# A graph layer and a GAT layer on one core: all rows of the second layer turned by VectorE, and ScalarE's opening order set by hand

## The chip, the cores and the metric

The kernel runs on one core of one Trainium2 chip. The time is device time in microseconds; the median of three runs of the kernel before is 937.41 us (936.95 to 938.42). The profiled execution that all rows below come from spans 936.6 us.

## The reference

There are 4096 nodes with 512 features. Layer 0 is attention inside 32 graphs of 128 nodes each (the tiles of the kernel), with the dense matrix `adj` standing for both biases; layer 1 is a graph attention layer with 8 heads over the edges `adj > 0`. Both are pre-norm with a residual:

```python
h = relu(layernorm(x))
q, k, v = h @ Wq.T + bq, h @ Wk.T + bk, h @ Wv.T + bv
a = where(same_graph, q @ k.T * scale, 0)
x = x + (softmax((a + adj + adj) * where(same_graph, 1, -1e6)) * same_graph) @ v

h = relu(layernorm(x))
mx = einsum('nf,hfd->hnd', h, W)                 # 8 heads of 64
t = einsum('hnd,hd->hn', mx, a_dst)              # s_i cancels in the softmax over j
attn = softmax(where(adj > 0, s_i + t_j, -inf))  # over j
x = x + concat_heads(attn @ mx)
```

So layer 1 is, for each node i, the sum over its neighbours j of exp(t_j) * mx_j, divided by the sum of exp(t_j). The kernel computes for each tile j of 128 nodes one "part", the weighted rows and their weights, split in a high and a low half for speed, and then multiplies the 0/1 mask with all 32 parts.

## The kernel before

It has three stages. Layer 0 walks over 16 groups of two tiles. In passing it reads all of `adj` (64 half-row tiles of 1 MB), sums exponentials of the entries outside the graph on ScalarE (`junk`), and lets VectorE write the mask as bytes to memory (`a_d`). A middle stage makes the parts of the tiles that layer 0 has not made yet. The aggregation multiplies masks and parts.

The opening folds the query and key weights into one matrix, `m_sb`:

```python
bq_sb = const.tile([P, KC], F32, name="bq_sb")
nc.scalar.dma_start(bq_sb, bq)
bk_sb = const.tile([P, KC], F32, name="bk_sb")
nc.scalar.dma_start(bk_sb, bk)
# ... (in fold)
wkT_sb = load_weight(tmp, wkT, "wkT_sb", KC, tag="lo")
wqT_sb = load_weight(tmp, wqT, "wqT_sb", KC, tag="lo")
loads()                       # first rows, wv, bv (ScalarE's queue), adjacency tiles
# ...
for n, wT in enumerate((wkT_sb, wqT_sb)):
    for k in range(KC):
        for m in range(KC):
            nc.tensor.transpose(pt[:, m, :], wT[:, k, ts(m, P)], ident)      # L198
        nc.scalar.copy(w[:, :, ts(k, P)], pt)
        if n == 0 and k == 0:
            rows = [spread_bias(b) for b in (bk_sb, bq_sb)]                  # L184
# ... VectorE: u_col, c_sb, zk from the weights and the bias rows
for m in range(KC):
    if m == 2: ...            # u_sb, z_sb (L224, L230)
    if m == 3: first()        # norm and turn the first two tiles
    for k in range(KC):
        nc.tensor.matmul(pp, wq[:, k, ts(m, P)], wk[:, k, :], ...)           # L236
    nc.scalar.mul(m_sb[:, m, :], pp, SCALE)                                  # L239
```

Then come `values` (L473) for the first two tiles, the reading of adjacency rows 0 and 1 (`read`: mask on VectorE, `junk` on ScalarE, own block on GpSimd) and `queries` (L461).

The rows of layer 1 (the output of layer 0, stored in `x1_d`) must be normalised, passed through a ReLU and transposed before the projection. Tiles 0 to 15 are transposed on TensorE:

```python
def relu_T(ps_pool, hn, dst):
    pt = ps_pool.tile([P, KC, P], F32, name="pt")
    for k in range(KC):
        nc.tensor.transpose(pt[:, k, :], hn[:, ts(k, P)], ident)             # L136
    nc.scalar.activation(dst, pt, AF.Relu)                                   # L137
```

Tiles 16 to 31 (`MIXED = NT // 2`) are transposed in 32 by 32 blocks by VectorE; four tiles share one block buffer, go to memory in one store, and come back with the blocks in place:

```python
def turn(i):
    c, b = divmod(i, BY)
    if b == 0:
        blocks[c] = sb4.tile([P, P // B, KC, BY, B], F32, name="blocks")
    nc.vector.transpose(blocks[c][:, :, :, b], rows[i].rearrange(...))       # L655
    if b == BY - 1:
        nc.sync.dma_start(hT_d[c], blocks[c]...)

def move(c):
    hT = sb5.tile([P, P // B, KC, P], F32, name="hT4")
    for q in range(P // B):
        nc.sync.dma_start(hT[ts(q, B)]..., hT_d[c, :, q]...)
    for u in range(BY):
        hTs[c * BY + u] = hT[:, u]
```

The projection and the weighting of one tile:

```python
def project1(ps_m, hT, w1x):
    pm = [ps_m.tile([P, D], F32, name="pp") for _ in range(2)]
    for g, n in ((1, HW + H), (0, HW)):
        for k in range(KC):
            nc.tensor.matmul(pm[g][:, :n], hT[:, k, :], w1x[:, k, g * HW : g * HW + n], ...)  # L264
    return pm
# weigh (L273, VectorE): e = pm * exp(t); split: high half (ScalarE), low half (GpSimd)
```

Layer 0's loop, cut to its order:

```python
for g in range(NG):                      # NG = 16
    s = scores(g, hT, gT, r, *look)      # L519
    prepare_on(last)
    if not last:
        ngT = queries(nhT)               # L461
    sT = turned(s)                       # L538
    prepare_on(3 <= g and g % 2)         # turn one row tile, project the one before
    for _ in range(...): begin1()        # fetch and norm a row tile
    for t in range(G):
        look_on(t)                       # read adjacency rows of group g + 1
        if not last and t == 0: nvs.append(values(nhT, t))
        attend(sT, vs[t], g, t)          # L546, writes x1_d
        prepare_on(last and t == 0)
        if not last and t: nvs.append(values(nhT, t))
    if g + 2 < NG:
        nhT, hns = turned0(g + 2)        # L136 for layer 0's own rows
        nr = row_terms(hns)
```

In the middle stage, for tiles below 16, TensorE turns the next row, and ScalarE weighs half of the tile in four pieces (L724); from 16 on VectorE weighs both halves. Rows to be turned by VectorE are taken up `AHEAD = 8` tiles before their projection; a move is issued three tiles before its first use.

## Time and profile before

| what | value |
|---|---|
| median time | 937.41 us |
| opening, to the first values product | 29.2 us |
| layer 0's groups | to about 355 us |
| middle stage (tiles 8 to 31) | 355.4 to 442.8 us |
| aggregation and end | 442.8 to 936.6 us |
| VectorE busy, 45 to 345 us | 204.74 us |
| ScalarE busy, 45 to 345 us | 175.93 us |
| DMA, 45 to 345 us | share 0.80, 308 GB/s |

The busy times come from the profile's table of windows. A DMA share of 1 means that all 16 DMA engines had packets the whole time. In the listings below a line gives the engine, the source line (L136), the operation, what it writes and reads, shapes, how often, and in brackets how long the engine stood idle before it and what released it; PE is TensorE, PEld its weight load, DVE VectorE, ACT ScalarE, POOL GpSimd, SP SyncE. A float32 product appears as two instructions, a transpose as one. The transposes by VectorE, and the costliest stores, in the page's columns (group, busy us and mean ns, idle before; for transfers the size and the median us from issue to landing):

```profile
L655 DVE STREAM_TRANSPOSE blocks<-rowm 128x512 f32<-128x512 f32 x16 | 11.2, 698 | 6.6 <-ACT rowm L730 6.5
a<-adj SPq DMA_DIRECT2D x64, 1024.0 KB, 12.2
a_d<-a SPq DMA_DIRECT2D x32, 512.0 KB, 10.3
hT_d<-blocks SPq DMA_DIRECT2D x4, 1024.0 KB, 4.6
hT<-hT_d SPq DMA_DIRECT2D x16, 256.0 KB, 5.2
```

### The profile page before, as it was taken

To read this page: it belongs to the slowest core of one execution; us is meant where nothing else is said; L and a number is where in the kernel's file an instruction comes from. 1 tells how busy PE (TensorE), PEld (TensorE's weight loads), DVE (VectorE), ACT (ScalarE), POOL (GpSimd) and SP (SyncE) were. 2 spreads that over 40 slices of the span, in tenths; PEclk is the share of its full clock that TensorE was granted. 3 is DMA by queue.
4 is the path that set the end of the run, shared out by engine and by line. 5 is a ranking of instruction groups with operands and counts; after the bars stand their busy time and mean duration, and the time that the engine had idled before them with its cause. 6 is when DMAs were issued, how large, how long until landed. Compare 5 with 4: busy or idle time off the path is not lost.

```text
span 936.6 us, 13145 instructions
## 1 busy us (share of the span) xinstructions
PE 925.9 (99%) x4987; PEld 809.1 (86%) x4987; DVE 462.2 (49%) x992; ACT 268.1 (29%) x539; POOL 180.4 (19%) x344
## 2 busy tenths in 40 slices
PE   8999999999999999999999999999999999999997
PEld 5676677767677778888999999999999999999997
DVE  4678878777775447754463324242424233332412
ACT  4876576667672216532000000000000000000000
POOL 1311212331221116654101010110101010101010
PEclk9999999999999999999999999999999999999999
DMA  9999997989997114764123131312121222313111
GB/s 334 415 382 401 349 351 302 360 344 371 356 354 273 35 35 146 203 200 103 53 61 91 46 90 46 90 51 85 52 85 54 82 71 65 88 48 90 46 45 37
DMA packets 61062, 156.63 MB, mean 167 GB/s; under 512 B 6722, under 2 KB 23490, under 8 KB 52290
## 3 DMA queue, kind: packets, MB, share of 16 engines
q1 hardware_dynamic: 51058, 138.70, 42.9%
q10 hardware_dynamic: 9936, 17.05, 4.9%
q8 instruction: 40, 0.66, 0.3%
q14 instruction: 28, 0.23, 0.1%
HBM read 117.97 MB, written 37.75 MB: 166 GB/s over the span
## 4 chain that ended last, share of the span: by engine, by line
PE 94%; DMA 3%; ACT 2%; DVE 0%; SPq 0%; issue 0%; ACTq 0%
PE pg L315 51%; PE pp L264 12%; PE pp L461 11%; PE pp L473 11%; PE pp L546 3%; PE pss L519 3%; DMA a<-adj 2%; PE pt L136 2%; ACT junk L496 1%; PE pl L315 1%; DMA bv_sb<-bv 1%; PE pss L538 0%; ACT m_sb L239 0%; ACT gT L465 0%; DVE x L548 0%
## 5 line engine op out<-in xcount | busy, mean ns | idle before, releaser
L315 PE MATMUL pg<-part,ata 128*128 128x348 f32 (+1 forms) x1536 | 246.7, 321 | 0.0
L315 PEld LDWEIGHTS pg<-part,ata 128*128 128x128 f32 x1536 | 244.5, 188 | 0.1
L315 PE MATMUL pg<-part,atb 128*128 128x348 f32 x1472 | 236.4, 321 | 0.0
L315 PEld LDWEIGHTS pg<-part,atb 128*128 128x128 f32 x1472 | 234.2, 188 | 0.1
L329 ACT COPY tot<-pg 128x522 f32<-128x522 f32 x31 | 18.6, 600 | 453.4 <-PE pg L315 453.4
L496 ACT ACTIVATE junk<-a 128x2048 bf16<-128x2048 f32 (+15 forms) x92 | 124.5, 1353 | 36.3 <-DMA a<-adj 15.1
L264 PE MATMUL pp<-w1x,hT 128*128 128x256 f32 (+1 forms) x512 | 114.9, 383 | 0.5 <-DVE e L273 0.5
L473 PE MATMUL pp<-wv,hT 128*128 128x512 f32 x256 | 115.0, 593 | 0.3 <-ACT hT L137 0.3
L461 PE MATMUL pp<-hT,m_sb 128*128 128x256 f32 x512 | 113.2, 379 | 0.0
L301 DVE CAST atb<-at 128x4096 fp32r<-128x4096 fp8e4 x16 | 36.7, 2293 | 152.2 <-PE pg L315 152.2
L264 PEld LDWEIGHTS pp<-w1x,hT 128*128 128x128 f32 x512 | 96.0, 190 | 15.0 <-issue 0.9
L461 PEld LDWEIGHTS pp<-hT,m_sb 128*128 128x128 f32 x512 | 96.1, 190 | 12.9 <-issue 0.5
L301 DVE CAST ata<-at 128x4096 fp32r<-128x4096 fp8e4 (+1 forms) x17 | 36.8, 2167 | 140.4 <-PE pg L315 140.3
L146 DVE TENSOR_SCALAR a<-a 128x512 fp8e4<-128x512 f32 x256 | 96.8, 457 | 5.7 <-DMA a_d<-a 5.7
L473 PEld LDWEIGHTS pp<-wv,hT 128*128 128x128 f32 x256 | 47.8, 190 | 54.9 <-issue 53.1
L767 POOL COPY den_all<-tot 128x1 f32<-128x1 f32 x31 | 5.8, 186 | 365.0 <-DVE tot L330 365.0
L771 POOL TENSOR_TENSOR tot<-tot,row 128x512 f32<-128x512 f32 x31 | 39.9, 1288 | 62.2 <-DVE tot L335 58.1
L248 POOL TENSOR_TENSOR part<-e,part 128x522 fp32r<-128x522 f32 x32 | 41.1, 1285 | 12.9 <-ACT part L245 12.7
L122 POOL TENSOR_SCALAR ve<-mv 128x1 f32<-128x1 f32 x64 | 16.3, 259 | 131.1 <-DVE mv L120 131.0
L137 ACT ACTIVATE hT<-pt 128x512 f32<-128x512 f32 x48 | 26.9, 596 | 50.8 <-PE pt L136 40.5
L477 DVE TENSOR_TENSOR v<-pp,bv_sb 128x512 f32<-128x512 f32 x32 | 22.0, 687 | 39.2 <-PE pp L473 39.2
L292 DVE STREAM_TRANSPOSE at<-mw 128x1024 f32<-128x1024 f32 x32 | 39.6, 1238 | 2.1 <-DMA mw<-a_d 2.1
(113 smaller groups left out, 698.4 us busy)
## 6 DMA issues: line engine op xcount, KB each, us to landing
a<-adj SPq DMA_DIRECT2D x64, 1024.0 KB, 12.2
a_d<-a SPq DMA_DIRECT2D x32, 512.0 KB, 10.3
mw<-a_d SPq DMA_DIRECT2D x128, 128.0 KB, 3.9
row<-x_d SPq DMA_DIRECT2D x41, 256.0 KB, 3.5
xg<-x SPq DMA_DIRECT2D x16, 512.0 KB, 5.1
x_d<-x ACTq DMA_DIRECT2D x32, 256.0 KB, 4.3
out<-tot ACTq DMA_DIRECT2D x31, 256.0 KB, 3.7
rowm<-x_d SPq DMA_DIRECT2D x16, 256.0 KB, 5.2
```

The source lines that it names most:

```text
L146: nc.vector.tensor_scalar(a8v[:, u], av[:, u], 0.0, None, ALU.is_gt, saturate=False)
L248: nc.gpsimd.tensor_sub(dst[:, :, 1, :], e3, dst[:, :, 0, :].bitcast(F32))
L264: nc.tensor.matmul(pm[g][:, :n], hT[:, k, :], w1x[:, k, g * HW : g * HW + n], start=(k == 0), stop=(k == KC - 1),)
L292: nc.vector.transpose(at8.rearrange("p c n b -> p (c n b)").bitcast(F32).rearrange("p (c u n) -> p c u n", c=NW, n=B), mw.rearrange("p u ( ...
L301: nc.vector.tensor_copy(at[:, c0 * BY : c1 * BY].rearrange("p (c b) q -> p c b q", b=BY), at8[:, c0:c1].rearrange("p c q b -> p c b q"),)
L315: nc.tensor.matmul(pg[:, : 2 * CW1].rearrange("p (s w) -> p s w", s=2)[:, :, :n], at[:, j, :], part(j)[:, c, :, :n], start=(j == 0), stop= ...
L461: nc.tensor.matmul(pp[:, : G * P], m_sb[:, k, ts(m, P)], hT[:, k, :], start=(k == 0), stop=(k == KC - 1),)
L473: nc.tensor.matmul(pp, hT[:, k, ts(t, P)], wv[:, k, :], start=(k == 0), stop=(k == KC - 1))
L496: nc.scalar.activation(junk[:, c0:c1], a[:, c0:c1], AF.Exp, scale=2.0 * NEG, accum_out=sums[:, n : n + 1],)
L519: nc.tensor.matmul(pss[:, t, :], gT[:, k, ts(t, P)], hT[:, k, ts(t, P)], start=(k == 0), stop=(k == KC - 1),)
L546: nc.tensor.matmul(po, sT[:, t, :], v, start=True, stop=True)
L771: nc.gpsimd.tensor_add(num, num, row)
```

## The change

All 32 row tiles of layer 1 are now turned by VectorE through memory, so that TensorE makes no transposes for layer 1. The first sixteen are turned inside layer 0: each group fetches a row tile at its start and takes it up at its end, one turn after the fetch could be used; stores and moves are placed by hand in chosen groups; the projections inside layer 0 sit in groups 7, 8, 9, 10 and 13 and three in the last. The order of TensorE in layer 0's groups is the program's. To make room, some of layer 0's buffers go from two to one (`gT`, `s`, `sT`) or from three to two (`diag`), and one of the seven adjacency tiles lives in a pool that stays on. In the opening the biases are loaded by SyncE behind the first weight (the value bias behind the value weight), TensorE runs ten transposes of the identity before the weights, the bias rows are spread after all of the first weight's transposes, and ScalarE's instructions follow the program's order until the first values, with the reading of adjacency rows 0 and 1 placed among the last products of the fold. The attention dot products of layer 1's weight (`dots`) are spread over four groups. `AHEAD` goes from 8 to 9. The branch for general inputs, which these inputs do not take, is adapted to the same row order.

```diff
-MIXED = NT // 2
-AHEAD = 8
+AHEAD = 9
+WARM = 10
@@
-    nc.scalar.dma_start(bq_sb, bq)
-    nc.scalar.dma_start(bk_sb, bk)
@@ mask_bytes
-        order = ("p (c b u q) -> p u c b q", "p (c u b q) -> p u c b q")[h]
-        av = a.rearrange(order, c=NW // 2, b=BY, q=B)
+        av = a.rearrange("p (c u b q) -> p u c b q", c=NW // 2, b=BY, q=B)
@@ fold
         wkT_sb = load_weight(tmp, wkT, "wkT_sb", KC, tag="lo")
+        nc.sync.dma_start(bk_sb, bk)
+        nc.sync.dma_start(bq_sb, bq)
         wqT_sb = load_weight(tmp, wqT, "wqT_sb", KC, tag="lo")
@@
+        pt = ps_t.tile([P, KC, P], F32, name="pt")
+        for _ in range(WARM):
+            nc.tensor.transpose(pt[:, 0, :], ident, ident)
@@
-                if n == 0 and k == 0:
+                if n == 0 and k == KC - 1:
                     rows = [spread_bias(b) for b in (bk_sb, bq_sb)]
@@ new: turning inside layer 0
+            keep = prep.enter_context(
+                tc.tile_pool(name="keep", bufs=1, side="right", reuse_waits="tile")
+            )
+            def turn(i, row, pool):
+                c, b = divmod(i, BY)
+                if b == 0:
+                    blocks[c] = pool.tile([P, P // B, KC, BY, B], F32, name="blocks")
+                nc.vector.transpose(blocks[c][:, :, :, b], row.rearrange(...))
+            def store(c): ...
+            def move(c):
+                hT = keep.tile(
+                    [P, P // B, KC, P], F32, name="hT4", tag="a" if c and c % 2 == 0 else "hT4"
+                )
+                ...
+            def fetch(i):
+                rows[i] = sb2.tile([P, D], F32, name="row1")
+                nc.sync.dma_start(rows[i], x1_d[i])
+            def begin(i):
+                norm(rows[i], rows[i])
+                nc.scalar.activation(rows[i], rows[i], AF.Relu)
+                turn(i, rows[i], keep)
@@ opening
+                def between(m, after):
+                    if m == 2 and not after:
+                        first.append(normed0(0))
+                        look[2].append(read(0, look[0][:, 0, :], look[1][0]))
+                    if m == 3 and not after:
+                        first.extend(turned0(0, first.pop()))
+                    if m == 3 and after:
+                        look[2].append(read(1, look[0][:, 1, :], look[1][1]))
+
+                with tc.manual_schedule(engines={mybir.EngineType.Activation}):
+                    m_sb, c_sb, u_sb, z_sb = fold(wp, lo, sb, ps_t, ps_p, loads, between)
@@ layer 0's loop
+                with tc.manual_schedule(engines={mybir.EngineType.PE}):
+                    for g in range(NG):
+                        for i in (g - 1, g) if last else (g - 1,) if g else ():
+                            fetch(i)
+                        if g in (6, 11, 14):
+                            move((6, 11, 14).index(g))
+                        ...
+                        if 2 <= g < 2 + KC:
+                            dots(g - 2)
+                        ...
+                        if g in (7, 8, 9, 10, 13, NG - 1):
+                            prepare()
+                        for t in range(G):
+                            look_on(t)
+                            if t == 0 and g in (5, 9, 13):
+                                store(g // BY - 1)
+                            ...
+                        for i in (g - 1, g) if last else (g - 1,) if g else ():
+                            begin(i)
+                store(LO // BY + 1)
@@ middle stage: every tile as the tiles from 16 on were
-                    if i + 1 < MIXED:
-                        hTs[i + 1] = sb2.tile([P, KC, P], F32, name="hT1")
-                        relu_T(ps_t, rows[i + 1], hTs[i + 1])
+                    if far <= NT:
+                        turn(far - 1, rows[far - 1], (keep, sb4)[(far - 1) // BY % 2])
+                        if far % BY == 0:
+                            store(far // BY - 1)
-                    if i < MIXED:
-                        halves = (0,)
-                        for h in range(H // 2, H):
-                            nc.scalar.mul(...)
```

## The prediction

> **What bounds the kernel now.** I read the page's busy shares first, then TensorE's own list of waits, then its instructions in order of time for the opening, for layer 0's groups and for the stage in between, because a share of 99% says only that the other engines cost nothing as long as they stay ahead. From the page:

> ```profile
> span 936.6 us, 13145 instructions
> PE 925.9 (99%) x4987; PEld 809.1 (86%) x4987; DVE 462.2 (49%) x992; ACT 268.1 (29%) x539; POOL 180.4 (19%) x344
> ```

> TensorE's idle time is 936.6 − 925.9 = 10.7 us. Its waits by releaser (total us, times, longest):

> ```profile
> PE pt L198 <- DMA wkT_sb<-wkT: 3.9, 1, 3.9
> PE pp L264 <- DVE e L273: 0.5, 1, 0.5
> PE pp L236 <- ACT m_sb L239: 0.3, 1, 0.3
> PE pp L473 <- ACT hT L137: 0.3, 1, 0.3
> ```

> That is 5.0 us; the remaining 5.7 us are the end, where the last product is evacuated, scaled and stored. Between 45 and 345 us TensorE is busy 299.86 of 300. So a gain must come from work taken off TensorE or from the opening, and everything added elsewhere is free only while TensorE still finds its data ready.

> The opening, TensorE in order of time (start, length, instructions, idle before):

> ```profile
> 3.92 1.08 PE L198 MATMUL pt<-ident,wkT_sb 128*128 128x128 f32 x4 [3.92 <-DMA wkT_sb<-wkT]
> 4.80 1.91 PE L184 MATMUL pp<-ident,bk_sb 128*128 128x128 f32 x8
> 6.51 1.91 PE L184 MATMUL pp<-ident,bq_sb 128*128 128x128 f32 x8
> 8.21 2.00 PE L198 MATMUL pt<-ident,wkT_sb 128*128 128x128 f32 x12
> 10.12 2.63 PE L198 MATMUL pt<-ident,wqT_sb 128*128 128x128 f32 x16
> 12.59 7.03 PE L236 MATMUL pp<-w,w 128*128 128x512 f32 x16
> ...
> 29.23 7.13 PE L473 MATMUL pp<-wv,hT 128*128 128x512 f32 x16 [0.29 <-ACT hT L137]
> ```

> Eight bias products take 6.51 − 4.80 = 1.71 us, 0.21 each; the same shape at 19.46 us (the row u, line 224) takes 0.89 for eight, 0.11 each. So TensorE works at half rate until about 8.9 us. From 12.59 to 29.23 lie 16.64 us, of which the work is 16.0 and waits for ScalarE 0.6.

> The stage between the layers, where layer 1's rows become weighted parts:

> ```profile
> 355.44 3.67 PE L264 MATMUL pp<-w1x,hT 128*128 128x264 f32 x16
> 358.95 0.60 PE L136 MATMUL pt<-ident,rown 128*128 128x128 f32 x4
> 359.39 3.67 PE L264 MATMUL pp<-w1x,hT 128*128 128x264 f32 x16
> ...
> 379.12 35.23 PE L264 MATMUL pp<-w1x,hT 128*128 128x264 f32 x160
> 414.86 28.29 PE L264 MATMUL pp<-w1x,hT 128*128 128x264 f32 x128 [0.51 <-DVE e L273]
> ```

> From start to start a tile costs 3.51 us of projection and, if TensorE turns it, 0.44 us for four transposes (359.39 − 358.95). The tiles from 379.12 on are turned by VectorE: no transposes.

> [...] first work at 3.92, full rate near 8.9. [...] VectorE's price is one transpose of 128x512 (0.698 us in this trace) and two transfers of 1 MB per four tiles. [...] with weights and biases on two queues the transfer rate falls to 131 GB/s between 4 and 5 us, with the engines still 64% busy. What can help is the order: weights first.

> **The change part by part.**
> (a) Transposes of layer-1 rows 0 to 15 leave TensorE: 16 tiles x 4 = 64 instructions. The trace has them as 36 of tile row (layer 0) and 28 of rown (after it). At 0.437/4 = 0.109 us each: 64 x 0.109 = 7.0 us, all on the bound engine, since it has no gap on either side. Nine tiles' share is inside layer 0 (3.9 us), seven tiles' after it (3.1 us).
> (b) VectorE gets 16 transposes of 0.70 us = 11.2 us, all in layer 0; seven more rows of statistics and normalising there (0.68 + 0.17 + 0.55 = 1.4 us each) = 9.8 us. Between 45 and 345 us it is busy 204.7 of 300 us (68%); with 21 more, 226 (75%). After layer 0 it loses those seven rows and gains the second half of the weighting for eight tiles (8 x 0.41 = 3.3 us, which ScalarE did in four pieces each, 0.93 us). ScalarE's ReLU merely changes its source: 0.60 us from PSUM, 0.63 from SBUF. All this lies beside TensorE: 0 us if it keeps ahead.
> (c) Transfers: four stores and three moves of 1 MB each and seven more rows of 256 KB come into layer 0, some 9 MB. The 308 GB/s x 300 us there are 92 MB; in the busiest windows at a DMA share of 0.99 to 1.02 the rate was 385 to 420. So the load goes from 0.80 to about 0.88: fits. The last adjacency tile is issued at 278.8 us and its users need it after 307, so 20 us of slack stand against some 22 us of transfer spread over 250.
> (d) The opening. The ten warm-up transposes can start when the identity is made (1.24 + 0.29 = 1.53 us) and, at 0.22 us cold, end at 3.8, before the first weights at 3.92: no cost, and 2.3 us of activity earlier. Biases behind the first weight mean that TensorE does the wkT transposes first. I estimate: wkT turned by 6.7 us, bias products done by 8.5, wqT transposes, paced by arrival, done by 10.5 in place of 12.5. Then 16.0 us of work, now with the two ScalarE waits (0.6 us) gone, because the order by hand puts m_sb and hT ahead of the mask sums of tile 1. That gives first values at about 26.5 in place of 29.2: 2.7 us. If transposes do not warm the clock, the bias products still run cold from 7.4 to 10.8 and only the 0.6 us and a little remain: 0.4. I weigh these 7 to 3: 2.0 us.
> (e) AHEAD 9 issues each four-tile move one tile (3.5 us) earlier. The 0.51 us stop at 414.86 is put down to VectorE's e, but the four PSUM tiles hold two tiles' products, so tile 24 needs tile 22's weighting, which ended at 411.3; I take it for a late move: gone, 0.5 us.
> (f) TensorE's order by hand in the groups: the trace already shows program order in every group (queries, turned scores, values, two attends, values), so 0. The mask's first half is read in the second half's order; its 256 operations last 0.45 us in either, so 0.
> (g) The aggregation, 3072 matmuls at about 159 ns, and the end: unchanged.
> Sum: 7.0 + 2.0 + 0.5 = 9.5 us; minus 0.2 for friction: 937.4 − 9.3 = 928.1, rounded to 928.

> **The rivals.**
> *The blocks buffer stops VectorE.* In layer 0 the turned blocks have one buffer: row 4's transpose must wait until the 1 MB store of rows 0 to 3 has been read. The store is placed in the middle of a group and the next transpose at its end, some 10 us later; layer 0's 512 KB mask stores take 10.3 us to land by the transfer table. VectorE works in order, so a wait there delays the v additions that free PSUM for TensorE. Against it: VectorE waited 39.2 us in layer 0 for TensorE's values, so it is that far ahead in places. If it bites at each of the three reuses plus row 16's, 1 to 3 us each: 931 to 936.
> *SyncE's queue is held by a move.* It waits for its store to land, and adjacency loads stand behind it. Seven half-row tiles are in flight, about 1.7 groups of 20 us, against a hold of some 10. If it bites: 2 to 4 us lost, 930 to 932.
> *The clock stays cold*: as in (d), 929.5.
> *VectorE becomes the pace after layer 0.* Tiles 8 to 15 now run at 3.51 us instead of 3.95 with all work on VectorE. In tiles of that kind before, it is busy 6.2 of 7.0 us in one window and 3.9 of 7.1 in the next, with a 2.2 us wait for a row every four tiles; TensorE did not stop for ten tiles. If it drifts over 15 tiles: 1 to 3 us lost.

> **Range and chances.** All gains are small beside 937: the most I can add is 7.0 + 3.9 (TensorE starting its products at 10 and never waiting) + 0.5, which gives 926.0, or 925.2 with the runs' own spread of some 0.8 us; two rivals together give 932. The eight-in-ten range is 925.2 to 931.8, longer above because every rival adds. Over 2% faster means under 918.7, which would need twice the removed work: 0.01. Over 2% slower means above 956, which needs a stop of over 1 us in every group of layer 0: 0.02. Within 2%: 0.97.

> **What would show it.** (a) TensorE has 128 + 0 row transposes at the turning line and busy time near 916 to 919. (d) The bias products take 0.11 us each, not 0.21, and first values start near 26.5; if they are still 0.21 the clock step fails. (e) One unbroken run of L264-type products from tile 8 to the aggregation, first aggregation product near 433. (b, c) TensorE's list of waits has nothing of over 0.5 us inside layer 0; an entry for VectorE's v, hn or s there speaks for the buffer, one for a transfer for the held queue. I would be wrong altogether if the aggregation's own spacing changed or layer 0's groups grew beyond the 18.4 us of a plain group now (62.35 to 80.72 from scores to scores; 21.9 with a prepared tile, 3.51 more).

## The result: 945.02 us, 0.7% longer

The changed kernel takes 945.02 us (median of 6 runs, 943.02 to 945.35), the kernel before 937.78 us in runs beside it (6 runs, 935.98 to 939.27). The ratio is 1.0074, with a 95% interval of 1.0060 to 1.0089. The prediction had said 928.0 us with a range up to 931.8. The page of the profiled execution:

```profile
span 943.2 us, 13085 instructions
PE 924.7 (98%) x4933; PEld 806.8 (86%) x4933; DVE 473.3 (50%) x1016; ACT 259.0 (27%) x507; POOL 174.3 (18%) x344
```

TensorE has 54 instructions fewer (64 row transposes gone, ten transposes of the identity added), and yet its busy time fell by only 1.2 us. Some of what is left must run slower. Its waits by releaser (total us, times, longest):

```profile
PE pt L135 <- DVE hn L129: 7.7, 5, 4.6
PE pp L502 <- ACT hT L136: 1.7, 2, 1.3
...
PE pp L271 <- issue: 1.3, 1, 1.3
```

Before, no entry of this list lay inside layer 0 except the 0.3 us at its start. Now TensorE waits there five times for `hn`, layer 0's own normalised rows, which it turns at each group's end (L135 is the turning, L136 its ReLU, L129 the normalising, L117 the statistics, L144 the mask, L271 the projection, L280 the weighting, L449 ScalarE's exponentials for it, L514 and L518 the values product and its bias, L560 the scores, L322 the aggregation; lines are those of the changed kernel). TensorE in order of time around the longest of them:

```profile
198.10 1.11 PE L135 MATMUL pt<-ident,hn 128*128 128x128 f32 x4 [4.61 <-DVE hn L129]
200.19 1.11 PE L135 MATMUL pt<-ident,hn 128*128 128x128 f32 x4 [0.98 <-DVE hn L129]
201.09 3.62 PE L560 MATMUL pss<-hT,gT 128*128 128x128 f32 x16
```

The sixteen score instructions take 3.62 us; in every undisturbed group they take 1.95. The table of windows shows why (window, then busy us and instructions of TensorE, its weight load, VectorE, ScalarE and GpSimd, granted TensorE clock, DMA share, GB/s):

```profile
194.00:196.00 2.00, 0.00 (x0) 0.00 (x0) 2.00 (x6) 0.98 (x2) 0.00 (x0) 0.90 0.84 287
198.00:200.00 2.00, 1.11 (x4) 0.71 (x4) 1.19 (x6) 0.60 (x1) 1.78 (x4) 0.50 1.05 440
202.00:204.00 2.00, 2.00 (x11) 2.00 (x11) 1.84 (x6) 1.97 (x4) 0.00 (x0) 0.50 1.13 448
204.00:206.00 2.00, 2.00 (x8) 1.73 (x7) 1.25 (x5) 0.78 (x5) 0.44 (x1) 0.54 0.95 393
```

While TensorE stood still the granted clock fell to 0.50, at 195.6 us, and it stayed there until 205.8 us. So the stop is paid twice: 4.61 us of standing still, and then 6.7 us of work at half rate.

**Where the 7 us are.** From the first values product to the first aggregation product the kernel before took 442.80 − 29.23 = 413.57 us, the changed one 448.58 − 27.64 = 420.94: 7.4 more, although 7.0 us of transposes are gone, so 14.4 us came in. The gaps in TensorE's list over that stretch, counted from start to start, add up to 11.4 us (0.5 in group 4 for `hT`, 0.7 at the end of group 6, 4.8 and 1.2 at that of group 7, 1.5 in group 9 for `hT`, 0.7 and 1.2 near 308 us, 1.4 at 406.6, minus the 0.6 of gaps that the kernel before had); the half clock after 198 us adds 3.2 (0.9 in the turning, 1.6 in the scores, 0.7 in the queries). That is 14.6. Opening and aggregation account for the rest: the opening is 1.6 us shorter, and the aggregation with the end is 0.9 us longer (494.6 us, before 493.7).

**What VectorE was doing.** In order of time, the changed kernel in group 7:

```profile
184.17 0.42 DVE L280 TENSOR_TENSOR e<-pp,e 128x256 f32<-128x256 f32 x1 [6.71 <-ACT e L449]
...
185.28 3.29 DVE L144 TENSOR_SCALAR a<-a 128x512 fp8e4<-128x512 f32 x6
...
194.13 1.11 DVE L144 TENSOR_SCALAR a<-a 128x512 fp8e4<-128x512 f32 x3
195.14 1.28 DVE L117 BATCH_NORM_STATS2 stats<-xg 128x6 f32<-128x512 f32 x2
...
197.49 0.55 DVE L129 TENSOR_SCALAR hn<-xg,mv,rstd 128x512 f32<-128x512 f32 x1 [0.42 <-POOL rstd L123]
```

and the kernel before in the same group:

```profile
179.90 0.68 DVE L118 BATCH_NORM_STATS2 stats<-xg 128x6 f32<-128x512 f32 x1
...
182.76 0.55 DVE L130 TENSOR_SCALAR hn<-xg,mv,rstd 128x512 f32<-128x512 f32 x1 [0.45 <-POOL rstd L124]
...
186.00 2.81 DVE L146 TENSOR_SCALAR a<-a 128x512 fp8e4<-128x512 f32 x8
```

Before, `x` was issued at 173.6 us and landed 4.7 later; its statistics came at 179.90, ahead of the masks, the second `hn` was done at 185.4, and TensorE wanted them at 198.4: 13 us in hand. In the changed kernel `x` was issued at 171.28 and landed after 10.3 us, at 181.6; but its statistics began at 195.14. In front of them VectorE stood idle until 184.17 for the exponentials of a projected tile, and then worked off the weighting, 14 mask operations and the values. TensorE wanted `hn` at 193.5. The data of the statistics lay unused for 13.5 us, from 181.6 to 195.14, behind this other work: VectorE kept to its order here. Nor was `x` itself what VectorE waited for. Its waits between 45 and 345 us, first in the kernel before, then in the changed one, which has no entry for `xg` at all:

```profile
DVE stats L118 <- DMA xg<-x: 9.0, 5, 3.7
DVE e L273 <- ACT e L414: 2.9, 4, 2.1
```

```profile
DVE e L280 <- ACT e L449: 15.7, 4, 6.7
```

VectorE's order is chosen when the kernel is built, and only TensorE's is fixed by hand in layer 0. VectorE's reads, with the mask's tile and count:

```
before, group 7:   stat stat hn hn | mask19 x8 | weigh weigh | mask20 x6 | v x1 x1 ...
changed, group 7:  mask17 x2 | weigh weigh | mask17 x6 | v x1 x1 | mask18 x8, v | stat stat hn hn
```

In the source `mask18` belongs to group 8.

**Second stop, in the middle stage.** VectorE in order of time, then TensorE:

```profile
404.69 0.69 DVE L117 BATCH_NORM_STATS2 stats<-row 128x6 f32<-128x512 f32 x1 [4.56 <-DMA row<-x_d]
406.13 0.71 DVE L280 TENSOR_TENSOR e<-pp,e 128x256 f32<-128x256 f32 x2
```

```profile
406.61 42.32 PE L271 MATMUL pp<-w1x,hT 128*128 128x264 f32 x192 [1.26 <-issue]
```

The rows to be turned stand in SyncE's queue behind the move of four turned tiles, and VectorE waited 4.56 us for one. Behind that wait, in VectorE's order, stood the weighting of tile 18, at 406.13. It frees the PSUM buffers that tile 20 takes over (four buffers, two to a tile), and TensorE's products for tile 20 began at 406.61. So this stop is of the same kind as the first: short work that TensorE needs, behind other work in VectorE's queue.

### The profile page after: what moved, and what is told of

Same layout as the page of the kernel before. It is cut to its first block, busy times and chain, and to the rows that moved or that the text cites. A ratio compares the mean times of both kernels' runs of the same rounds, so it can differ in the third digit from the quotient of the medians.

```text
span 943.2 us, 13085 instructions
## 1 busy us (share of the span) xinstructions
PE 924.7 (98%) x4933; PEld 806.8 (86%) x4933; DVE 473.3 (50%) x1016; ACT 259.0 (27%) x507; POOL 174.3 (18%) x344
## 4 chain that ended last, share of the span: by engine, by line
PE 94%; DVE 2%; POOL 1%; ACT 1%; issue 1%; DMA 0%; SPq 0%; ACTq 0%
PE pg L322 51%; PE pp L271 12%; PE pp L502 12%; PE pp L514 10%; PE pss L560 3%; PE pp L587 3%; PE pp L242 1%; PE pt L135 1%; PE pl L322 1%; POOL rstd L123 1%; DMA wkT_sb<-wkT 0%; DVE hn L129 0%; POOL ve L121 0%; PE pss L579 0%; DVE stats L117 0%
## 5 line engine op out<-in xcount | busy, mean ns | idle before, releaser
L322 PE MATMUL pg<-part,ata 128*128 128x348 f32 (+1 forms) x1536 | 246.8, 321 | 0.0
L322 PEld LDWEIGHTS pg<-part,ata 128*128 128x128 f32 x1536 | 244.5, 188 | 0.1
L322 PE MATMUL pg<-part,atb 128*128 128x348 f32 x1472 | 236.8, 321 | 0.0
L322 PEld LDWEIGHTS pg<-part,atb 128*128 128x128 f32 x1472 | 234.6, 188 | 0.1
L537 ACT ACTIVATE junk<-a 128x2048 bf16<-128x2048 f32 (+15 forms) x92 | 124.3, 1351 | 22.6 <-DVE x L589 13.5
L271 PE MATMUL pp<-w1x,hT 128*128 128x256 f32 (+1 forms) x512 | 113.9, 383 | 1.3 <-issue 1.3
L514 PE MATMUL pp<-wv,hT 128*128 128x512 f32 x256 | 114.9, 592 | 0.0
L271 PEld LDWEIGHTS pp<-w1x,hT 128*128 128x128 f32 x512 | 96.7, 190 | 17.0 <-issue 2.3
L144 DVE TENSOR_SCALAR a<-a 128x512 fp8e4<-128x512 f32 x256 | 97.9, 463 | 3.1 <-DMA a_d<-a 2.8
L514 PEld LDWEIGHTS pp<-wv,hT 128*128 128x128 f32 x256 | 47.9, 190 | 54.3 <-issue 53.8
L280 DVE TENSOR_TENSOR e<-pp,e 128x256 f32<-128x256 f32 x64 | 25.0, 408 | 37.1 <-ACT e L449 26.0
L121 POOL TENSOR_SCALAR ve<-mv 128x1 f32<-128x1 f32 x64 | 18.4, 292 | 133.9 <-DVE mv L119 133.8
L518 DVE TENSOR_TENSOR v<-pp,bv_sb 128x512 f32<-128x512 f32 x32 | 21.9, 684 | 35.0 <-PE pp L514 35.0
## 6 DMA issues: line engine op xcount, KB each, us to landing
a<-adj SPq DMA_DIRECT2D x64, 1024.0 KB, 11.4
```

The costliest lines, as they stand in the source:

```text
L144: nc.vector.tensor_scalar(a8v[:, u], av[:, u], 0.0, None, ALU.is_gt, saturate=False)
L322: nc.tensor.matmul(pg[:, : 2 * CW1].rearrange("p (s w) -> p s w", s=2)[:, :, :n], at[:, j, :], part(j)[:, c, :, :n], start=(j == 0), stop= ...
L514: nc.tensor.matmul(pp, hT[:, k, ts(t, P)], wv[:, k, :], start=(k == 0), stop=(k == KC - 1))
L537: nc.scalar.activation(junk[:, c0:c1], a[:, c0:c1], AF.Exp, scale=2.0 * NEG, accum_out=sums[:, n : n + 1],)
```

## The experiments

The expectations use four names. ORDER: the work is the same, only its place in VectorE's fixed order makes `hn` late. LOAD: VectorE or the transfers have too much to do in layer 0. BUFFER: one buffer less (`diag`, or the turned blocks) holds VectorE up. ARRIVAL (in the first run TRANSFER): `x`, with three buffers, lands too late for any order. All ratios are to runs of the kernel before on the same chip, with 95% intervals.

### VectorE's order by hand

The first edit puts VectorE's instructions of layer 0's groups in the program's order too, with a program order made for it: first mask, then the statistics and normalising of the tiles two groups on and of layer 1's row, then the other masks, about 6 us into the group.

```diff
-with tc.manual_schedule(engines={PE}):
+with tc.manual_schedule(engines={PE, DVE}):
@@ group
+    mask(first tile)
+    fhns = [norm(xg[g + 2][:, t]) for t in range(G)];  norm(rows[g - 1])
     masks(other tiles) ... values, attends ...
-    nhT, hns = turned0(g + 2);  begin(g - 1)
+    nhT, hns = turned0(g + 2, fhns)
```

> The changed kernel with all its work, but VectorE's order in layer 0's groups set by hand: scores, first half of the first mask, row sums, second half, then the statistics and normalising of the tiles two groups on, and only then the second mask, the weighting, the sums and the values. Theory ORDER (in the changed kernel the normalising stands behind the masks and the weighting, so TensorE's transposes find no data, idle 4.6 us once, and TensorE then works at half clock for 6 us): no wait for hn of over 0.5 us is left, no stretch of half clock after the opening, and the time falls by the 9.4 us of waits for hn and hT and the 3.2 us of half clock, to 931 to 934. Theory LOAD (VectorE has 21 us more work in layer 0 than fits): the waits stay, at other places, with the same sum of 8 to 12 us, time 942 to 946. Theory TRANSFER (the tile x comes late because SyncE's queue is held): the statistics wait for xg on VectorE by 2 us or more in several groups, and the time stays above 938.

The second moves that one block, statistics and normalising, to the end of the group and leaves the rest.

> The same hand order as the run before with one block moved: statistics and normalising of the tiles two groups on, and of the layer-1 row, stand at the end of the group, behind both masks and the values. Theory ORDER: TensorE waits for hn in nearly every group, since VectorE can start on it only after the second values product, so some 2 to 4 us of wait in each of 14 groups and stretches of half clock: 970 to 1010. Theory LOAD: the amount of work is the same as in the run before, so within 4 us of its time.

They (e1 and e2) took 957.75 us (954.86 to 960.0; ratio 1.021, 1.0178 to 1.0242) and 1028.6 us (1026.8 to 1032.7; 1.0991, 1.0957 to 1.1025). With the same work and the same buffers, the place of one block (and of the turning that follows on it) is worth 71 us. TensorE's waits with the block late:

```profile
PE pt L135 <- DVE hn L129: 50.6, 15, 3.6
```

So a late normalising can cost much more than the loss to be explained, and more than the 970 to 1010 us expected. But the early place was no cure: `x` was issued at 80.56 us and used at 90.60, at 120.59 and used at 131.30, and VectorE, told to take it at 6 us, waited 47.9 us in 13 places for it, with everything else behind it, as TRANSFER had said; ORDER's 931 to 934 missed. ORDER and ARRIVAL both had a part in this run; the next ones try to separate them.

A third takes `x` a group earlier (four buffers in place of three, one `v` buffer less) and stores turned blocks right after the fourth transpose.

> VectorE's order by hand as in the first run, where it stood idle 43 us for x tiles and 10.7 us for the block buffer; now x tiles are loaded a group earlier (four buffers instead of three, paid for by three instead of four buffers of v), and each store of turned blocks is issued right after its fourth transpose. Theory ORDER AND ARRIVAL (the work fits, what cost time was waiting in a fixed order for transfers issued too late): VectorE's waits for xg and for the block buffer fall below 5 us together, TensorE has no wait of over 1 us in layer 0 and no half clock after the opening, 929 to 934. Theory LOAD (the added 21 us do not fit): TensorE still waits 8 us or more in layer 0 for VectorE's results, 940 or more.

This one (e5) took 948.92 us (947.84 to 949.87; 1.0129, 1.0112 to 1.0145). The waits for `x` were down to 7.7 us in 3 places, and VectorE now waited 50.6 us for layer 1's row, whose statistics stood just as early while the row itself is fetched at the group's start. A fourth puts `x`'s block half way through the group and the row's at its end, with three buffers again, and a fifth gives it four buffers and the two mends of the middle stage described below.

> The changed kernel, three x buffers as it has, VectorE's order in layer 0 written by hand: the first tile's mask first, then the first halves of the other three masks, then the statistics and normalising of the tiles two groups on (about half way through the group, so some 6 us ahead of the turned store that needs them), the second halves of the masks and the row of layer 1 at the end, the store right after the fourth turn. ORDER (only the place of the normalising in VectorE's fixed order cost the time): no wait of TensorE for hn over 0.5 us in layer 0, no half clock there, 934 to 939, with the stop at tile 20 (some 2 us) still in it. ARRIVAL (with three buffers x lands 7 to 10 us into a group, and any order then stalls): VectorE waits 2 us or more for xg in many groups, TensorE waits for hn or for the weights, 940 or more.

> The hand order of the last kernel with x fetched a group earlier (four x buffers), the middle stage's rows one tile further ahead, and the turned blocks of tiles 16 to 19 in the other block buffer. ORDER: as good as the tool's own order with those three edits (933.08), 930 to 934. ARRIVAL: the stalls of the three-buffer kernel are gone here, so the difference between the two is over 5 us after some 2 to 3 us for the middle stage.

They (e13 and e14) took 946.03 us (942.56 to 948.33; 1.0087, 1.0062 to 1.0113) and 943.91 us (943.6 to 946.48; 1.008, 1.0063 to 1.0097). With three buffers no wait of TensorE for `hn` was left at all, as ORDER had it, but the time missed its 934 to 939; VectorE waited 21.2 us in 8 places for `x`, and TensorE for the weighting, as ARRIVAL had it. Four buffers took the waits for `x` down to 5.9 us in 2 places, but the step brought only about 2 us, as much as the middle stage's mends alone, and so missed both. TensorE now stops for the weighting, which these orders had put too late (e13, its waits):

```profile
PE pp L599 <- DVE e L280: 6.7, 2, 3.7
PE pp L507 <- ACT hT L136: 2.9, 2, 2.1
```

Each of the five hand orders moved the stop and none removed it. My orders were poor, and they do not settle whether `x` comes too late for a good one.

### x a group earlier, with one v buffer less

```diff
-v = sb.tile([P, D], F32, name="v", bufs=4)
+v = sb.tile([P, D], F32, name="v", bufs=3)
-xg[g] = sb.tile([P, G, D], F32, name="xg", bufs=3)
+xg[g] = sb.tile([P, G, D], F32, name="xg", bufs=4)
-        load_pair(g + 2)
+        load_pair(g + 3)          # in group 0 also g + 2
```

> The changed kernel with only the x tiles loaded a group earlier (four buffers, v three); VectorE's order is again what the placing tool makes. Theory ARRIVAL alone (hn late because x comes late): the 7.7 us of waits for hn vanish and with them the half clock, 932 to 935. Theory ORDER (hn late because VectorE waits 6.7 us for a projection's exponentials in front of the masks): waits of 3 us or more stay in group 7 or move to another engine's list, 938 to 946.

This one (e6) took 937.24 us (936.0 to 937.93, 12 runs; 0.9999, 0.9990 to 1.0008): some 7 us less than the changed kernel. VectorE's order was made anew when this kernel was built: the statistics of a pair of tiles now stand about a group ahead of their use. In group 7, VectorE's lines and then TensorE's:

```profile
168.15 0.68 DVE L117 BATCH_NORM_STATS2 stats<-xg 128x6 f32<-128x512 f32 x1
171.77 1.12 DVE L129 TENSOR_SCALAR hn<-xg,mv,rstd 128x512 f32<-128x512 f32 x2
```

```profile
191.99 1.04 PE L135 MATMUL pt<-ident,hn 128*128 128x128 f32 x8
```

The normalised rows lie ready 19 us before TensorE takes them. All waits for `hn` and the half clock in layer 0 are gone. The windows of the changed kernel and of this one, from 45 to 345 us (columns as above):

```profile
45.00:345.00 300.00, 290.64 (x1214) 202.85 (x1213) 215.91 (x570) 176.76 (x346) 63.80 (x143) 0.98 0.89 330
```

```profile
45.00:345.00 300.00, 299.70 (x1276) 210.21 (x1275) 220.49 (x582) 178.82 (x352) 65.45 (x146) 1.00 0.90 332
```

VectorE does more in these 300 us (220.5 against 215.9), the transfers run as full (0.90), and TensorE stands still 0.3 us in place of 9.4. This refutes LOAD. VectorE still waits for a projection's exponentials in group 7 (6.89 us at 182.09), but now behind the normalising, where it does no harm. The waits for `hn` went, as this run's ARRIVAL had said and its ORDER had not. But the edit does two things at once: `x` lands earlier, and the build places its normalising earlier. What was left was one stop of 3.26 us at the start of the middle stage, again with a half clock after it.

### Buffers

```diff
-sb.tile([P, G, P], F32, name="diag"),            # two buffers
+sb.tile([P, G, P], F32, name="diag", bufs=3),
```

> The changed kernel with one number restored: three buffers for the own blocks (diag) in place of two. Theory BUFFER: with two, GpSimd's copy of the own block waits for the scores of two groups before (13 waits, 72 us together in the changed kernel, 3 and 26 us in the kernel before), the adjacency tile stays occupied, its successor is loaded later, and VectorE gets its masks just in time instead of early, so the last mask is written at 334 us instead of 291 and every group's normalising queues behind masks. With three buffers the copy's waits fall below 30 us, the last mask ends before 310 us, the waits for hn vanish, no half clock, and the time is 930 to 936. If the buffer is not the cause (the added work or the x tiles are): waits for hn of 5 us or more stay, 942 to 946.

> The kernel before with the opposite edit: two buffers for the own blocks in place of three, nothing else. Theory BUFFER alone: the copy's waits grow to 60 us or more, the last mask moves from 291 to 320 us or later, TensorE begins to wait in layer 0, and the time rises to 940 to 945. If the buffer matters only together with the added 21 us of VectorE's work: masks later as well, but no wait of TensorE over 1 us, 937 to 938.5. If it matters not at all: masks end at 291 us as before.

With `diag` back at three the changed kernel (e9) takes 943.0 us (942.63 to 943.79; 1.0063, 1.0047 to 1.0078), with every wait as it was (7.7 us for `hn`, the longest 4.61). The kernel before with two (e10) takes 936.89 us (0.9996, 0.9987 to 1.0004); GpSimd, which fills that buffer, then waited 95 us for it, and TensorE waited for nothing in layer 0 but the 0.2 us at its start. The third run also moves the turned blocks of tiles 16 to 19 to the other block buffer, and includes the mend of the middle stage.

```diff
-turn(far - 1, rows[far - 1], (keep, sb4)[(far - 1) // BY % 2])
+turn(far - 1, rows[far - 1], (sb4, keep)[(far - 1) // BY % 2])
```

> The changed kernel with three mends: three diag buffers, rows of the middle stage fetched one tile further ahead, and the turned blocks of tiles 16 to 19 put into the other block buffer, so that VectorE does not wait for the last store of layer 0. If theory BUFFER holds and the two stops of the middle stage are late transfers: no wait of TensorE over 0.6 us after the opening, 927 to 931 (the 928 of the prediction). If the buffer is not the cause: 940 or more.

This one (e11) took 942.1 us (941.67 to 943.14; 1.0052, 1.0039 to 1.0066), 7.7 us of waits for `hn` as ever. BUFFER is refuted for `diag` and for that block buffer; `gT`, `s` and `sT` have one buffer in the fast version above too.

### Parts of the change alone

TensorE's order in layer 0 left to the build:

```diff
-with tc.manual_schedule(engines={PE}):
+if True:
```

> The changed kernel without the hand order of TensorE in layer 0's groups; the placing tool then moves the scores of group 8 ahead of the transposes that wait in group 7. Theory ORDER, with TensorE's fixed order as a part of it: the 4.6 us wait shrinks by the 2 us of scores that fill it, the clock does not fall to half, and the time is 936 to 940. If TensorE's fixed order has no part: 944 to 946, with the 4.6 us wait and the half clock in place.

This one (e3) took 949.82 us (948.4 to 951.6; 1.0134, 1.0109 to 1.016), longer than with the hand order, and outside both expectations: the waits for `hn` are as many (five) and shorter (the longest 1.8 us), those for `hT` are more (five in place of two), and the clock falls to half twice. The order by hand is not what costs.

The kernel before with the new opening and nothing else:

> The kernel before with the new opening alone: biases behind the first weight, ten warm-up transposes, ScalarE's order by hand until the first values. All theories: first values product at 27.6 us as in the changed kernel (29.2 before), and the time lower by 1.6 us, 935.5 to 936.5. If the opening disturbs what follows (the first masks are read in another order), the gain is gone by the first aggregation product and the time stays at 937 to 938.

This one (e4) took 935.86 us (934.66 to 937.99, 20 runs; 0.9984, 0.9977 to 0.9991): 0.8 to 2.2 us gained.

The middle stage's rows fetched one tile further ahead:

```diff
-load(far + 2)
+load(far + 3)
```

> The changed kernel with the rows of the middle stage fetched one tile further ahead, so that one more row is on its way when SyncE's queue is held by a move. Theory for the 1.3 us stop at tile 20: rows stuck behind the move make VectorE wait 2.8 and 4.6 us for a row, so that the next store and move are late. Then these waits fall below 1 us, the stop is gone, and the time falls by 1.3 us to 943 to 944. If the stop comes from the move's own length (store and move take over 11 us of a 14 us period), it stays: 945.

This one (e7) took 942.97 us (942.85 to 943.22; 1.0066, 1.0049 to 1.0082): the stop at 406.61 is gone and layer 0's waits are the same to 0.01 us.

The changed kernel without the ten transposes of the identity (`WARM = 0`):

> The changed kernel without the ten warm-up transposes. If transposes warm the clock: full rate comes 2.4 us later, about 10 us instead of 7.7, the bias products last 0.21 us each again, first values product at 28.3 to 29 instead of 27.6, time 1 us higher. If transposes do not warm it: the same opening, first values at 27.6, time unchanged within 0.5 us.

This one (e8) took 946.02 us (945.0 to 948.13; 1.0102, 1.0083 to 1.0121). This run can't answer for the clock: its opening was even shorter (first values at 26.31 us, because the first weights' last quarter landed sooner), and the longer time is a longest wait for `hn` of 6.0 us in place of 4.6. It was repeated in a version without that wait, below.

### The version that beats both

`x` a group earlier, rows one tile further ahead, and the block buffers exchanged:

> The kernel with x tiles a group earlier (937.2 us, with a 3.3 us stop and 3 us of half clock at the start of the middle stage) and the two mends of the middle stage: further rows, other block buffer for tiles 16 to 19. The stop there came from VectorE's transpose of row 16 waiting 1.6 us for the last store of layer 0 and then 4.6 us for a row behind the move. Then it and its half clock are gone: 929 to 932. If the stop comes from the weighting itself being too much for VectorE: 936 to 938.

This one (e12) took 933.08 us (932.71 to 933.69, 5 runs; 0.9955, 0.9942 to 0.9969), between the two ranges expected. On the same chip, the version that differs in having three `x` buffers (four of `v`, and `diag` at three) took 942.1: the earlier `x` is worth 9.0 us. The list of waits of TensorE has one line of size left:

```profile
PE pp L271 <- DVE e L280: 2.1, 1, 2.1
```

The next version takes up the last two rows of layer 0 before the last group's attends, to remove that stop; the one after it also drops the ten transposes.

```diff
 if g in (7, 8, 9, 10, 13, NG - 1): prepare()
+if last:
+    for i in (g - 1, g): begin(i)
```

> The version with x a group earlier, rows one tile further ahead and turned blocks to the other buffer (933.08 us, one wait of 2.1 us left, for the weighting at the start of the middle stage), with the last two rows of layer 0 taken up before the attends of the last group. ORDER: the 2.1 us stop shrinks below 0.5 and the time is 930.5 to 931.5. If that stop only moves to another place of VectorE's order: 932.5 to 933.5.

> The version before it without the ten transposes of the identity at the start. WARM (they bring TensorE to full clock before the first weights land, as the prediction weighted with 0.7): the bias products again at some 0.21 us each and the time 0.6 to 1.5 us longer. ORDER OF THE OPENING (the new order of ScalarE and of the loads made the gain): the time within 0.4 us of the version with them, or shorter.

The first (e15) took 932.7 us (932.18 to 933.69; 0.9956, 0.9943 to 0.997): not to be told from the one before, the stop of 2.1 us became one of 2.6, but the 3.4 us of half clock that followed it before did not come. Why that stop stays is open. Without the ten transposes (e16) it is 935.82 us (933.31 to 937.22, 21 runs; 0.9979, 0.9971 to 0.9987). TensorE's opening with them:

```profile
6.15 0.63 PE L205 MATMUL pt<-ident,wkT_sb 128*128 128x128 f32 x4 [0.52 <-DMA wkT_sb<-wkT]
...
27.08 7.03 PE L514 MATMUL pp<-wv,hT 128*128 128x512 f32 x16
```

and without them:

```profile
6.08 1.12 PE L205 MATMUL pt<-ident,wkT_sb 128*128 128x128 f32 x4 [0.49 <-DMA wkT_sb<-wkT]
...
27.78 7.03 PE L514 MATMUL pp<-wv,hT 128*128 128x512 f32 x16
```

The same four transposes take 0.63 us against 1.12 at the same moment, so the ten do bring TensorE to its full rate sooner: by the trace's record of the clock at 5.64 us in place of 8.98. Until then TensorE had done nothing but transposes (18 in e15), so the clock rose after transposes alone, which the prediction had left open. In the 16 traces with the ten, full rate began between 4.54 and 7.85 us, in the four without them between 6.54 and 9.32. Their worth is 0.7 us of opening here. The profiled spans are 2.1 us apart (930.3 and 932.4); most of the rest is three waits of TensorE for ScalarE's `hT` in layer 0 (1.7 us in all against 0.3), whose place shifts with the opening.

### One place in the order, with three buffers

The last pair changes one thing in VectorE's order as the build makes it: no mask of a group's tiles stands ahead of the normalising that the group before has to hand over. Three `x` buffers stay. The second of the two has the mends of the middle stage.

```diff
+normed[g] = norm(xg[g][:, t, :], hn).ins
@@ read
-    mask_bytes(a8, a, h)
+    with tc.issue_after(normed[g + 1]):
+        mask_bytes(a8, a, h)
```

> The changed kernel with one rule added to VectorE's order in layer 0: no mask of a group's tiles goes ahead of the normalising of the tiles that the group before it has to turn (as the source has them). Three x buffers, the same work, all else left as it is. ORDER (the normalising waits behind masks that are not yet needed): the 4.61 us wait for hn in group 7 falls below 0.5 us and so does the half clock after it, so about 7 us less: 936 to 939, with the stop at tile 20 (some 2 us) still there. ARRIVAL (x comes too late with three buffers): VectorE waits for xg itself, the hn waits stay over 2 us, 941 or more.

> The same rule, with the rows of the middle stage one tile further ahead and the turned blocks of tiles 16 to 19 in the other block buffer, to set beside the version with four x buffers (933.08 us) and the one with three and no rule (942.1 us). ORDER: 932.5 to 936, within 3 us of the four-buffer version. ARRIVAL: 939 or more.

They (e17 and e18) took 943.64 us (941.34 to 945.22; 1.0058, 1.0043 to 1.0073) and 941.17 us (940.24 to 943.12; 1.0044, 1.0031 to 1.0057). The wait in group 7 fell from 4.61 to 3.60 us only. VectorE in that group (e17):

```profile
193.11 0.69 DVE L518 TENSOR_TENSOR v<-pp,bv_sb 128x512 f32<-128x512 f32 x1 [2.68 <-PE pp L514]
193.72 1.28 DVE L117 BATCH_NORM_STATS2 stats<-xg 128x6 f32<-128x512 f32 x2
```

The masks are gone from the front of the statistics, and VectorE stands idle in their place, for 2.68 us, because the values' addition `v` stands in front too and its product was not done. `x` had been issued at 172.7 and had landed 10.0 us later, at 182.7: 11 us unused. So ORDER's numbers missed (936 to 939, and 932.5 to 936), since I had named only one of the things that stand in front. ARRIVAL's numbers came true (941 or more, and 939 or more), but its mark, a wait of VectorE for `x` itself, is not there in this group either.

## Why the prediction was wrong, step by step

**(a) The transposes, −7.0.** Right. 64 transposes are gone from TensorE. In the version of 932.7 us the stretch from first values to first aggregation is 435.80 − 27.08 = 408.7 us; without its one stop of 2.6 us that is 406.1, which is the 413.6 of before less 7.0 and less the 0.5 us stop it had.

**(b) VectorE's added work lies beside TensorE, "0 us if it keeps ahead".** This is the step that failed. The sum was good (215.9 us busy in the changed kernel and 220.5 with `x` earlier, where I had 226), and it is no measure of keeping ahead. What counts is when one short chain, statistics, GpSimd's two steps, normalising, comes up in VectorE's order. That had 13 us in hand before and came 4.6 us late after. I read VectorE's wait of 39.2 us for the values as "it is that far ahead in places", though such a wait is a part of the queue in front of everything behind it; e17 shows the same kind of wait, 2.68 us, in front of `hn`. The loss by it is 10.6 us of gaps in layer 0 and 3.2 of half clock. The gaps for `hT` belong to it: before the one in group 9 ScalarE had waited 5.70 us for VectorE to normalise layer 1's row, and `hT` stood behind that in ScalarE's order. That an earlier `x` takes the loss away is shown (9.0 us, e12 against e11). Why the build placed the chain so late with three buffers is not.

**(c) The transfers fit.** Right: a share of 0.89 where I had 0.88, and with the same transfers the version with `x` earlier has no stop in layer 0 but 0.3 us. They are not free either: in group 7 `x` took 10.3 us to land in place of 4.7. This alone stopped nobody in the changed kernel.

**(d) The opening, −2.0.** Right within the scatter of arrivals: 1.6 us in the profile, 1.3 alone (e4), 2.2 and 2.5 in the versions of 932.7 and 933.08; the old opening itself took 28.04 us instead of 29.23 in e10. (In the kernel before, full rate began at 9.28 us by the record of the clock, not near 8.9.) The 0.7 weight on a warm clock, my estimate, was on the right side; the term is 0.7 us, not 2.3. The rest, 1.5 us against the profiled kernel before but only 0.3 against e10, is the order of loads and of ScalarE.

**(e) AHEAD 9 removes the 0.5 us stop.** Wrong. That stop went, but a new one of 1.26 us came at tile 20, because each move that goes out earlier goes out ahead of rows that VectorE still needs, in one queue, and VectorE's wait for such a row (4.56 us) held up the weighting behind it. I looked at the user of the move and not at what stands behind it. One tile further ahead for the rows mends it (e7).

**(f) Orders by hand cost nothing.** Right for TensorE's order, which gains some 5 us against the order the build makes (e3). But it has a side that I did not see: for the changed kernel VectorE's order was made anew, and I took it to stay as it was. Fixing TensorE's order is not what spoilt it: without that (e3) the waits for `hn` are as many.

**The rivals.** The one that named VectorE named the wrong cause, a buffer (e9 to e11 refute it), and took a wait of TensorE for `hn` as its sign. The sign came, from data that lay ready and unused. The held queue came true in the middle stage, not in layer 0, and with it the size of the rival that had VectorE as the pace there (1 to 3 us for a wait for a row every four tiles): 1.26 us at tile 20. The range ended at 931.8 because I had let two rivals add up to 932 and no rival made a stop longer than its own wait; the half clock did, by 3.2 us.

What is not settled: whether an order exists that does with three `x` buffers what the build makes with four. Three orders by hand and one rule with three buffers did not find it, and two orders by hand with four were no better. ORDER and ARRIVAL are therefore not fully parted: in the changed kernel `x` lay ready, but the cure that worked was to fetch it earlier. That less work on VectorE would have helped was not tried.

## What to carry to other kernels

When work moves to an engine with spare time, look for the engine's short hand-overs (here the normalised rows) and ask of each how long its result lies ready before its user takes it (13 us before, 19 with `x` earlier): that time, not the busy share, says how much may be put in front of it. If the result comes late, the time that its input lay ready (13.5 us here) tells a bad place in the order from a late input. Whoever fixes one engine's order by hand should read the order of the others again. An input fetched one group earlier, for one buffer, lets the build place the chain early, and here was worth more (9.0 us) than the transposes the change had removed (7.0).

## What was unexpected of the hardware

A stop of TensorE can cost more than its length: after 4.61 us of idling the clock was at 0.50 until 205.8 us, which cost another 3.2. Shorter stops also did it, and not each time: 2.10 us (e12 and, at 284.8 us, e13) were followed by half rate, 2.09 us (e14) and 2.59 us (e15) were not.
